# Eight more score halves fetched at the switch between two stages of a four-layer graph network, into tiles that the first stage has done with

## The chip, the core and the metric

The kernel runs on one core of a Trainium2 chip. The metric is the device time of one execution in microseconds (us), as the median of several runs. A profile is one execution with the hardware profiler on; its span goes from the first to the last instruction, and the execution's own time is a little longer.

The engines are PE (matmul), DVE (vector), ACT (activations), POOL (GpSimd) and SP, which here only issues DMAs. All large transfers of this kernel are issued by SP and share the core's 16 DMA engines.

## What is computed

The reference applies four graph layers with a residual each to `x` of 128 batches x 128 nodes x 128 features, with an integer adjacency `adj`. The change concerns the second layer, whose attention scores come from the absolute difference of every pair of nodes:

```python
D = jnp.abs(x[:, :, None, :] - x[:, None, :, :])
h = jnp.einsum('bijc,oc->bijo', D, W1) + b1          # 64 outputs for each pair
m = jnp.mean(h, axis=(0, 1, 2))
v = jnp.mean((h - m) ** 2, axis=(0, 1, 2))           # over ALL batches and pairs
h = (h - m) / jnp.sqrt(v + EPS) * g1 + be1
h = _leaky(h)
s = jnp.einsum('bijo,uo->biju', h, W2)[..., 0] + b2[0]
A = jax.nn.softmax(jnp.where(A_init > 0, s, NEG), axis=-1)
```

The mean and variance run over all batches, so no score can be finished before `h` of every pair is known. The kernel therefore computes `h` for all batches in a first stage and comes back to it in a second one.

## The kernel before, in words

**First stage.** The 128 batches stand in 32 groups of four (`G` = 4, `NG` = 32, `NB` = 128). For each group a "chain" (`chain(g)` in the first stage, lines 427 to 549) does layer one with tiles `x`, `adj`, `mask`, `hn`, `hT`, `maskT`, `hw`, `o` and `h1` of pool `p0`. For each batch, `pairs(i)` (lines 378 to 401) makes four steps `i`: a difference of 128x2048 in a tile `d` (two tiles for DVE, two for POOL: tags `d0` and `d1`, two buffers each, line 322), its absolute value on ACT, the product with `W1` on PE, a copy from PSUM on ACT into a half of a tile `z`, and statistics on DVE. Two steps fill one half of a batch: 128x2048 float32, 1 MB, 8 KB a partition. The half is written to DRAM (`HP`, line 359). The halves live in a ring of `FETCHED` = 10 tiles `z` (line 656).

**The order.** The steps of the first stage carry an engine, a cost, their predecessors and a rank. `_ranked` lays them out in one order, and each engine's instructions stand in it in that order. SP is one such queue: an instruction that waits on it holds back all that stand behind it.

**The switch.** The last four batches (n = 0 to 3 in the order of the second stage) are never written to DRAM: their eight halves stay in the ring. The step `fetch` (line 686) fetches the next batch (n = 4: two halves, `HP[0]`) into the two tiles left. In between stands a short block of small instructions (lines 727 to 762) that turns the statistics into `scale1` and `bias1`.

**Second stage.** It runs in slots, `slot(b)` (lines 843 to 877) with b from -1 on, in an order written out by hand. Slot b prepares batch b + 1 on ACT (`z0`, line 850, and `zr`, line 854) and DVE (`z0`, line 868), multiplies batch b on PE (line 825, 24 matmuls), copies the sums of batch b - 1 (`su`, line 846), brings them into order on PE (line 832) and adds them to `sk` (lines 839, 841). Then it fetches one batch, b + 5, into the two ring tiles that batch b has just left (lines 875 and 876, `fetch` at line 658, the DMA at line 662).

Every four slots one group's scores are complete, and a "turn" of the second stage's own `chain(turn)` (lines 879 to 977) does the rest of layer two for it, with its steps placed at fixed slots. For turn k: in slot 4k + 5 SP writes `sk` to DRAM (`rows<-sk`, line 902) and loads `x` (line 905); in slot 4k + 7 SP reads the scores back in another layout (`u<-rows`, line 909), which waits until `rows` has landed; in slot 4k + 9 DVE normalises `x` (line 244) and folds `u` (line 920); in slot 4k + 10 PE transposes `u` (line 894) and DVE makes the scores (lines 924, 925); in slots 4k + 11 to 4k + 16 softmax and products follow, with tiles `hT`, `aT` and `yT` (line 897). The result goes to DRAM (lines 957, 958), except for the groups of turns 27 to 31 (`KEPT` = 5), whose `Y` and `X1` stay on chip in a pool `keep` of ten small tiles.

From slot 12 to slot 38 some steps of `brief()` (preparations for the last stage) stand in the slots too; in slots 21 to 36 these are two maxima over a byte mask on DVE in each slot.

**Last stage.** Layers three and four, group by group, behind a condition computed on the way (`bounded`). The functions `last_stage` and `two_stages(True)` belong to branches of which the profile has no instruction.

Of the kernel before, what the change touches and what calls it, by code (L numbers as in the profile page):

```python
# [9 lines left out]
F32 = mybir.dt.float32  # L10
# [7 lines left out]
P = 128  # L18
G = 4
# [9 lines left out]
KC = 8  # L29
ROW = P + 2 * KH  # L30
# [3 lines left out]
NT = KH // KC  # L34
KEPT = 5
# [134 lines left out]
def tile_gnn_stack(ctx: ExitStack, tc: tile.TileContext, a: dict, out: bass.AP):  # L170
    nc = tc.nc
    NB = a["x"].shape[0]
    NG = NB // G
# [5 lines left out]
    psum, banks, Y, X1 = None, {}, {}, {}  # L179
# [44 lines left out]
    MV1 = res.tile([P, NG, G, 2], F32, name="MV1")  # L224
# [41 lines left out]

    def two_stages(general):
        nonlocal psum, banks
        early, middle, early_ring = (ExitStack() for _ in range(3))
        psum = early.enter_context(tc.tile_pool(name="psum", bufs=1, space=bass.MemoryType.PSUM))  # L270
        banks = {"sm": 2}
        ahead_by = FETCHED - 2 * general
# [1 line left out]
        with tc.tile_pool(name="c0", bufs=1) as c0, tc.tile_pool(name="p0", bufs=2) as p0:  # L274
# [42 lines left out]
            def difference(i):  # L317

                b, t = divmod(i, NT)
                xe, k = XE[b // 2], b % 2  # L320
                on_pool = t in ON_POOL
                d = p0.tile([P, 2, KC, P], F32, tag=f"d{int(on_pool)}", bufs=2 - general, name="d")
                x = xe[:, k, 0:P] if on_pool else XP[b // 2 % 2][:, k, :]
                ahead = xe[:, k, 1 + KC * t:]
                ahead = bass.AP(tensor=ahead.tensor, offset=ahead.offset,
                                ap=[list(ahead.ap[0]), [KH, 2], [1, KC], [1, P]])
                eng = nc.gpsimd if on_pool else nc.vector
                eng.tensor_tensor(d, ahead, x[:, None, None, :].to_broadcast([P, 2, KC, P]),  # L328
                                  OP.max if t == BY_MAX else OP.subtract)
                diffs[i] = d.rearrange("p h k i -> p h (k i)")  # L330
# [96 lines left out]
            def chain(g):  # L427
# [4 lines left out]
                own = lambda *names: [(name, g) for name in names]  # L432

                def tile0(name, dtype=F32, **kw):
                    t[name] = p0.tile([P, G, P], dtype, tag=name, name=name, **kw)
                    return t[name]

                def loaded():
# [70 lines left out]

                def h1(half):  # L510
                    if g not in H1:
                        H1[g] = p0.tile([P, G, P], F32, name="h1", bufs=3)
                    for k in (2 * half, 2 * half + 1):
                        nc.scalar.activation(H1[g][:, k, :], t["x"][:, k, :], AF.Relu, bias=t["nb"][:, k:k + 1],
                                             scale=t["rs"][:, k:k + 1])
# [129 lines left out]
            if general:  # L645
# [3 lines left out]
                steps.clear()  # L649
                relations()  # L650

            ring = early_ring.enter_context(tc.tile_pool(name="ring", bufs=1, side="right"))
            fetched = []

            def held_z():
                return ring.tile([P, NT // 2 * KC * P], F32, tag="z", bufs=ahead_by, name="z")

            def fetch(n):

                if n < 2 * NB:  # L660
                    b, half, z = n // 2 - G, n % 2, held_z()
                    nc.sync.dma_start(z, HP[b][:, half * NT // 2:(half + 1) * NT // 2, :].rearrange("p a b -> p (a b)"))
                    fetched.append(z)

            def first_fetches():
                fetched.extend(halves[b, half] for b in range(NB - G, NB) for half in range(2))
                for n in range(2 * G, ahead_by):
                    fetch(n)

            pick = fixed([P, 2, 8], F32, name="pick")  # L670
            nc.gpsimd.tensor_copy(pick.rearrange("p h (a c) -> p h a c", a=2),
# [11 lines left out]
                chain(g)  # L683
            for i in range(NT * NB):
                pairs(i)
            step("fetch", "SP", 0.8, [("hs", NT * NB - 2), ("st", NT * NB - 2 * NT), ("out", NB - G - 1)], NT * NB, first_fetches)
            later = []

            def in_const(name, *parts, n=P, shape=None):
# [73 lines left out]


        early.close()
        if not general:
            keep = ctx.enter_context(tc.tile_pool(name="keep", bufs=1))
            for g in range(NG - 1 - KEPT, NG - 1):
                Y[g], X1[g] = (keep.tile([P, G, P], F32, name=f"{n}{g}") for n in ("y", "x1"))
        psum = middle.enter_context(tc.tile_pool(name="psum2", bufs=1, space=bass.MemoryType.PSUM, reuse_waits="tile"))  # L770
        banks = {"ps": 3, "pk": 2, "sm": 3}
        with tc.tile_pool(name="c1", bufs=1, reuse_waits="tile") as c1, \
                tc.tile_pool(name="p1", bufs=2, reuse_waits="tile") as p1:
            prepared, scored = {}, {}

            z0 = c1.tile([P, 1], F32, name="z0")
            nc.vector.scalar_tensor_tensor(z0, bias1, 0.01, bias1, op0=OP.mult, op1=OP.max)
# [65 lines left out]
            def slot(b):  # L843
                if b - 1 in scored:
                    su = p1.tile([P, 4, P], F32, name="su")
                    nc.vector.tensor_copy(su.rearrange("p a b -> p (a b)"), scored[b - 1])  # L846
                    scored[b - 1] = su, sm("pk", "pk")
                if b + 1 < NB:
                    z0, z1 = fetched.pop(0), fetched.pop(0)
                    nc.scalar.activation(z0, z0, AF.Identity, bias=bias1, scale=scale1[:, 0:1])  # L850
                now(b, "am")
                if b + 1 < NB:
                    zr = p1.tile([P, NT // 2 * KC * P], F32, name="zr", bufs=3)
                    nc.scalar.activation(zr, z1, AF.Relu, bias=bias1, scale=scale1[:, 0:1])  # L854
                    prepared[b + 1] = z0, z1, zr
                now(b, "e")
                if b in prepared:
                    z0b, z1b, zrb = prepared.pop(b)
                    ps = psum.tile([P, 512], F32, tag="ps", bufs=banks["ps"], name="ps")
                    products(ps, [(w2z, z0b)], 0)  # L860
                    products(ps, [(w2l, z1b)], 4)
                if b - 1 in scored:
                    by_k(b - 1)
                if 0 <= b < NB:
                    products(ps, [(w2r, zrb)], 4)
                    scored[b] = ps
                if b + 1 < NB:
                    nc.vector.scalar_tensor_tensor(z0, z0, 0.01, z0, op0=OP.mult, op1=OP.max)  # L868
                now(b, "p")
                now(b, "a")  # L870
                if b - 1 in scored:
                    to_sk(b - 1)
                now(b, "l")
                if 0 <= b < NB:
                    fetch(2 * b + ahead_by)
                    fetch(2 * b + ahead_by + 1)
                now(b, "s")

            def chain(turn):
# [14 lines left out]
                        nc.tensor.transpose(t[name][:, k, :], src[:, k, 0:P], ident)  # L894

                def copied(name, src):
                    t[name] = p1.tile([P, G, P], F32, tag=name, name=name)
                    nc.scalar.copy(t[name], t[src])

                def to_rows():  # L900
                    to = rows[0, 0, 0:1]
                    nc.sync.dma_start(bass.AP(tensor=to.tensor, offset=to.offset,
                                              ap=[[ROW + 1, P], [P * ROW, G], [1, 1 + 2 * KH]]), own_sk)
                    t["x"] = p1.tile([P, G, P], F32, name="x", bufs=3)
                    nc.sync.dma_start(t["x"], X[g])

                def from_rows():
                    t["u"] = p1.tile([P, G, ROW], F32, name="u")
                    nc.sync.dma_start(t["u"], rows.rearrange("g i r -> i g r"))

                def normed():
                    t["h"] = pre_norm(p1, t["x"], MV1[:, g], RS1[:, g])
                    t["cap"] = p1.tile([P, G, P], F32, name="cap")
                    nc.gpsimd.tensor_scalar(t["cap"], M8[g], BIG, NEG12, op0=OP.mult, op1=OP.add)
                    t["x1"] = X1[g] if g in Y else p1.tile([P, G, P], F32, name="x1", bufs=3)
                    nc.gpsimd.tensor_tensor(t["x1"], t["x"], over_group(bt), OP.add)  # L916

                def folded():
# [1 line left out]
                    nc.vector.tensor_tensor(u[:, :, 0:2 * KH], u[:, :, 0:2 * KH], u[:, :, P:], OP.add)  # L920

                def scores():
                    t["e"] = p1.tile([P, G, P], F32, name="e1")
                    nc.vector.tensor_tensor(t["e"], t["u"][:, :, 0:P], t["put"], OP.add)
                    nc.vector.tensor_tensor(t["e"], t["e"], t["cap"], OP.min)

# [21 lines left out]
                    nc.tensor.matmul(t["pz"], wgT, t["yT"], start=True, stop=True)  # L948

                def biased():  # L950
                    t["y"] = Y[g] if g in Y else p1.tile([P, G, P], F32, name="y")
                    nc.scalar.activation(t["y"], t["pz"], AF.Identity, bias=bg)

                def stored():
# [168 lines left out]


        middle.close()
        early_ring.close()

    two_stages(False)
# [4 lines left out]
    def last_stage():  # L1133
        nonlocal psum, banks
        with tc.tile_pool(name="c2", bufs=1) as c2, tc.tile_pool(name="p2", bufs=5) as p2, \
# [84 lines left out]
            def group(g):  # L1220
# [27 lines left out]
                for k0 in range(0, G, 2):  # L1248
# [13 lines left out]
                    yield from last_of(softmax(pes), got)  # L1262
                    eTs = []
                    for e in got[0]:
                        eT = p2.tile([P, 4, P], F32, name="eT", bufs=12)
                        transpose(eT, e)
                        eTs.append(eT)
                        yield
# [26 lines left out]
                sums = small.tile([P, 1, G], F32, name="sums3")  # L1295
                got = []
                yield from last_of(softmax([pe], sums), got)
                eT = p2.tile([P, 4, P], F32, name="eT", bufs=12)
                transpose(eT, got[0][0])
                nc.vector.reciprocal(sums, sums)  # L1300
                yield
# [332 lines left out]
```

## Time and profile before

| | |
|---|---|
| median of 3 runs | 2674.77 us (2673.55 to 2675.49) |
| the profiled execution: its own time | 2676.09 us |
| its span | 2674.2 us, mean granted PE clock 0.98 |
| busy share: PE, DVE, ACT, POOL | 91%, 92%, 89%, 64% |
| moved by DMA | 611.43 MB; read 312.58 MB, written 296.03 MB |
| fetches `z<-hp` / writes `hp<-z` | 248 each, 1024 KB each, median 13.7 / 4.0 us from issue to landing |
| `u<-rows`, `rows<-sk` | 32 each, 384 KB and 130 KB, median 11.4 and 13.0 us |
| last result copy of the first stage on ACT (line 352) | starts at 1450.6 us |
| first preparation on ACT (line 850) | starts at 1459.3 us |
| first and last batch's first matmul (line 825) | 1463.8 and 2211.2 us |
| first instruction of the last stage on ACT (line 1373) | 2247.03 us |

In a row of the profile, `L825 PE MATMUL ps<-z,w2z` is line 825, its engine, operation, and the tile written and those read; `SPq` is SP issuing a DMA. "Idle <-X" is the time that the engine stood idle just before, and what ended it. A row such as `DVE u L920 <- DMA u<-rows: 30.0, 17, 5.7` of the view of waits reads: who waited for whom, us in all, times, the longest. The view of windows gives for each stretch of time the busy us of each engine (and instructions), the granted PE clock, the mean busy share of the DMA engines and GB/s.

### The profile page before, as it was taken

Reading aid. Unit: us, or ns where it says so; the run is one execution under the profiler, and the core shown is the slowest. Engines: PE = TensorE matmul, PEld = TensorE weight load, DVE = VectorE, ACT = ScalarE, POOL = GpSimd, SP = SyncE. Lnnn points to the kernel's source line nnn. Section 1 sums busy time; section 2 is a strip of 40 time slices with the busy share of each in tenths; the row PEclk is TensorE's granted clock in tenths of the full one; section 3 lists DMA queues with packets and bytes.
Section 4 is the critical chain, followed back from the end, with each engine's and each line's share of the span. In section 5 each row is a group of like instructions: output and inputs, shape, how many; then the busy total and the mean of one; then the engine's idle time right before and its main releaser. Section 6 shows DMA issues by size and latency. Waiting matters only on the chain.

```text
span 2674.2 us, 41925 instructions
## 1 busy us (share of the span) xinstructions
PE 2437.0 (91%) x14521; PEld 1162.1 (43%) x14521; DVE 2469.6 (92%) x4738; ACT 2380.3 (89%) x2821; POOL 1706.1 (64%) x1628
## 2 busy tenths in 40 slices
PE   6999999999999999999997988888888886999997
PEld 3333333333333333333332443444444445777776
DVE  5999999999999999999998789988888886899997
ACT  5999999999999999999998877788778874999997
POOL 6999999999999999999985000010101123666663
PEclk8999999999999999999998999999999998999999
DMA  3555555555555555555542999999999992021211
GB/s 101 201 206 209 212 212 211 212 213 205 209 205 209 205 210 204 217 204 216 205 197 93 409 409 384 392 409 410 411 410 411 410 373 81 21 68 56 64 37 34
DMA packets 185426, 611.43 MB, mean 229 GB/s; under 512 B 31987, under 2 KB 99702, under 8 KB 121718
## 3 DMA queue, kind: packets, MB, share of 16 engines
q1 hardware_dynamic: 184768, 608.50, 59.1%
q8 instruction: 118, 1.93, 0.3%
q14 instruction: 102, 0.84, 0.1%
q10 hardware_dynamic: 438, 0.17, 0.0%
HBM read 312.58 MB, written 296.03 MB: 228 GB/s over the span
## 4 chain that ended last, share of the span: by engine, by line
PE 37%; ACT 24%; DVE 15%; DMA 12%; POOL 7%; issue 4%; SPq 0%; POOLq 0%; DVEq 0%; ACTq 0%
PE hp L338 16%; ACT d L376 9%; ACT z L352 7%; DMA z<-hp 4%; PE hp L341 4%; DMA rows<-sk 4%; PE ps L825 4%; POOL d L328 4%; DMA u<-rows 3%; DVE z L868 3%; ACT o L473 2%; PE pk L832 2%; ACT hn L473 2%; PE xp L414 1%; DVE e L1502 1%
## 5 line engine op out<-in xcount | busy, mean ns | idle before, releaser
L328 POOL TENSOR_TENSOR d<-xe 128x2048 f32<-128x2048 f32 x256 | 1073.8, 4205 | 36.4 <-PE hp L338 34.5
L338 PE MATMUL hp<-d,w1T 128*64 128x512 f32 x4096 | 994.1, 601 | 57.6 <-ACT z L352 54.5
L376 ACT ACTIVATE d<-d 128x2048 f32<-128x2048 f32 x384 | 733.8, 1924 | 19.8 <-POOL d L328 19.5
L328 DVE TENSOR_TENSOR d<-xe,xp 128x2048 f32<-128x2048 f32 x256 | 583.6, 2280 | 7.0 <-POOL xe L423 4.0
L352 ACT COPY z<-hp 128x1024 f32<-128x1024 f32 x512 | 519.1, 1015 | 9.7 <-PE hp L338 4.5
L338 PEld LDWEIGHTS hp<-d,w1T 128*64 128x64 f32 x4096 | 276.9, 136 | 559.5 <-issue 455.3
L916 POOL TENSOR_TENSOR x<-x,bt 128x512 f32<-128x512 f32 x32 | 48.8, 1525 | 665.7 <-DMA x<-x 494.1
L366 DVE BATCH_NORM_STATS2 st<-z 128x6 f32<-128x512 f32 x512 | 354.7, 693 | 6.2 <-ACT z L352 6.1
L367 DVE BATCH_NORM_STATS2 st<-z 128x6 f32<-128x512 f32 (+1 forms) x512 | 336.4, 657 | 0.0
L868 DVE SCALAR_TENSOR_TENSOR z<-z 128x2048 f32<-128x2048 f32 x128 | 299.5, 2340 | 5.5 <-ACT z L850 5.3
L850 ACT ACTIVATE z<-z,bias,scale 128x2048 f32<-128x2048 f32 x128 | 267.5, 2090 | 8.9 <-DVE bias L762 7.7
L854 ACT ACTIVATE zr<-z,bias,scale 128x2048 f32<-128x2048 f32 x128 | 267.7, 2092 | 0.5 <-DMA z<-hp 0.5
L341 PE MATMUL hp<-both_t,xw 128*64 128x512 f32 x1024 | 265.2, 592 | 0.0
L825 PE MATMUL ps<-z,w2z 128*32 128x512 f32 x1024 | 140.9, 622 | 61.2 <-DVE z L868 60.5
L832 PEld LDWEIGHTS pk<-pick,su 128*128 128x128 f32 x1024 | 126.8, 195 | 147.8 <-DVE su L846 112.9
L832 PE MATMUL pk<-pick,su 128*128 128x16 f32 x1024 | 139.4, 268 | 34.6 <-DVE su L846 33.8
L825 PE MATMUL ps<-zr,w2r 128*32 128x512 f32 x1024 | 142.5, 629 | 0.0
L341 PEld LDWEIGHTS hp<-both_t,xw 128*64 128x64 f32 x1024 | 77.6, 137 | 142.2 <-issue 142.2
L825 PE MATMUL ps<-z,w2l 128*32 128x512 f32 x1024 | 138.4, 610 | 0.0
L1525 PE MATMUL pv<-wr,e 128*128 128x128 f32 x1024 | 134.0, 278 | 2.1 <-ACT wr L1450 1.1
L1525 PEld LDWEIGHTS pv<-wr,e 128*128 128x128 f32 x1024 | 124.1, 192 | 8.4 <-ACT wr L1450 1.8
L1409 ACT ACTIVATE h<-x,nb,rs 128x128 f32<-128x128 f32 x256 | 106.0, 491 | 20.1 <-POOL nb L1404 18.4
(241 smaller groups left out, 3808.3 us busy)
## 6 DMA issues: line engine op xcount, KB each, us to landing
hp<-z SPq DMA_DIRECT2D x248, 1024.0 KB, 4.0
z<-hp SPq DMA_DIRECT2D x248, 1024.0 KB, 13.7
x<-x SPq DMA_DIRECT2D x118, 256.0 KB, 4.8
u<-rows SPq DMA_DIRECT2D x32, 384.0 KB, 11.4
x<-in_x_dram SPq DMA_DIRECT2D x32, 256.0 KB, 5.6
adj<-in_adj_dram SPq DMA_DIRECT2D x32, 256.0 KB, 5.9
out_dram<-x SPq DMA_DIRECT2D x32, 256.0 KB, 2.4
z<-y SPq DMA_DIRECT2D x27, 256.0 KB, 11.8
```

What stands on the lines that cost most here:

```text
L328: eng.tensor_tensor(d, ahead, x[:, None, None, :].to_broadcast([P, 2, KC, P]), OP.max if t == BY_MAX else OP.subtract)
L338: nc.tensor.matmul(hp[64 * hh:64 * hh + 64, c:c + 512], w1T2 if by_max else w1T, d[:, hh, c:c + 512], start=True, stop=not by_max, skip_gr ...
L341: nc.tensor.matmul(hp[64 * hh:64 * hh + 64, c:c + 512], XW[i // NT // 2][:, i // NT % 2, :], both_t.rearrange("p h k i -> p h (k i)")[:, h ...
L352: nc.scalar.copy(half_of(b, t), linear.pop(i))
L366: nc.vector.bn_stats(st[:, 2 * t, :], hs[:, 0:512])
L367: nc.vector.bn_stats(st[:, 2 * t + 1, :], hs[:, 512:1024 - P * last])
L376: nc.scalar.activation(diffs[i], diffs[i], AF.Abs)
L825: nc.tensor.matmul(ps[32 * c:32 * c + 32, :], w[:, w0:w0 + 32], v[:, 512 * c:512 * c + 512], start=j0 == 0, stop=w is w2r, skip_group_chec ...
L832: nc.tensor.matmul(pk[:, kk, 0:16], su[:, kk, :], pick.rearrange("p h j -> p (h j)"), start=True, stop=True)
L850: nc.scalar.activation(z0, z0, AF.Identity, bias=bias1, scale=scale1[:, 0:1])
L854: nc.scalar.activation(zr, z1, AF.Relu, bias=bias1, scale=scale1[:, 0:1])
L868: nc.vector.scalar_tensor_tensor(z0, z0, 0.01, z0, op0=OP.mult, op1=OP.max)
```

## The change

It lets eight more halves be fetched at the switch. The first stage's chain tiles move into a pool of their own, `upper`, and the difference tiles into another, `spare`. Once the last group's chain is done, four halves (n = 4 and 5) are fetched over the chain tiles; the ring's two free tiles take n = 6; and as the last four differences are used up, four halves (n = 7 and 8) go into the tiles `d`. So five batches are asked for ahead of slot 0 instead of one.

In the slots the fetches are rearranged (`refill`): slots 0 to 3 fetch n = 9 to 12, slots 4 and 5 nothing, slot 6 n = 13, slot 7 n = 14 (into two of the tiles `d`, from here on called the pair), slot 8 nothing, slot 9 n = 15, and so on with n = b + 6; every sixth slot from 14 to 104 uses the pair. Slot 110 fetches nothing, and from slot 111 on n = b + 5. After slot 5 the space of the chain tiles goes to the turns (`x`, `u`, `hn`, `cap`, `x1`, `e1`, `y`); after slot 8 two of the tiles `d` serve as `hT`, `aT`, `yT` (two of each) and as two of the ten kept tiles; after slot 110 the pair holds the other eight.

The number of instructions of SP, PE and ACT's and DVE's large ones is the same. In the built order, SP's four fetches over the chain tiles stand ahead of the two last writes of the first stage (`hp123`); POOL's first `cap` stands behind `scale1` instead of ahead of it; and DVE's `w2r` and `add_k` stand after line 754 of before instead of among lines 736 to 739.

```diff
-                d = p0.tile([P, 2, KC, P], F32, tag=f"d{int(on_pool)}", bufs=2 - general, name="d")
+                d = room["d"].tile([P, 2, KC, P], F32, tag=f"d{int(on_pool)}", bufs=2 - general, name="d")
...
-                    t[name] = p0.tile([P, G, P], dtype, tag=name, name=name, **kw)
+                    t[name] = room["chain"].tile([P, G, P], dtype, tag=name, name=name, **{"bufs": 2} | kw)
...
+            room = {"d": p0, "chain": p0}
+            if not general:
+                room["d"] = ctx.enter_context(tc.tile_pool(name="spare", bufs=1, side="right"))
             ring = early_ring.enter_context(tc.tile_pool(name="ring", bufs=1, side="right"))
-            fetched = []
+            if not general:
+                room["chain"] = upper.enter_context(tc.tile_pool(name="upper", bufs=1, side="right"))
+            fetched, asked = {}, itertools.count(G)
...
-            def fetch(n):
-                if n < 2 * NB:
-                    b, half, z = n // 2 - G, n % 2, held_z()
-                    nc.sync.dma_start(z, HP[b][:, half * NT // 2:(half + 1) * NT // 2, :].rearrange("p a b -> p (a b)"))
-                    fetched.append(z)
+            def fetch(pair):
+                n = next(asked)
+                if n < NB:
+                    fetched[n] = pair = [next(pair), next(pair)]
+                    for half, z in enumerate(pair):
+                        nc.sync.dma_start(z, HP[n - G][:, half * NT // 2:(half + 1) * NT // 2, :].rearrange("p a b -> p (a b)"))
+            in_ring = (held_z() for _ in itertools.count())
+            def spares():
+                for _ in range(2):
+                    for tag in ("d0", "d1"):
+                        yield room["d"].tile([P, 2, KC, P], F32, tag=tag, bufs=2, name="z").rearrange("p h k i -> p (h k i)")
+            in_spares = (z for _ in itertools.count() for z in spares())
+            def upper_pool(name):
+                upper.close()
+                return upper.enter_context(tc.tile_pool(name=name, bufs=1, side="right", reuse_waits="tile"))
+            def upper_fetches():
+                room["chain"] = None
+                pool = upper_pool("upper_z")
+                pairs = (pool.tile([P, NT // 2 * KC * P], F32, name=f"z{n}") for n in range(4))
+                fetch(pairs)
+                fetch(pairs)
             def first_fetches():
-                fetched.extend(halves[b, half] for b in range(NB - G, NB) for half in range(2))
-                for n in range(2 * G, ahead_by):
-                    fetch(n)
+                fetched.update({b - NB + G: [halves[b, 0], halves[b, 1]] for b in range(NB - G, NB)})
+                for n in range(2 * G, ahead_by, 2):
+                    fetch(in_ring)
+            def spare_fetches():
+                fetch(in_spares)
+                fetch(in_spares)
...
+                step("upper", "SP", 0.8, [("xp", 2 * g), ("xp", 2 * g + 1), ("h1", g, 0), ("h1", g, 1), ("x", g)], NT * NB, upper_fetches)
+                step("spare", "SP", 0.8, ["fetch", ("hp", NT * NB - 1)], NT * NB, spare_fetches)
+            step("fetch", "SP", 0.8, [("hs", NT * NB - 2), ("st", NT * NB - 2 * NT), ("out", NB - G - 1)] + in_upper, NT * NB, first_fetches)
...
-            keep = ctx.enter_context(tc.tile_pool(name="keep", bufs=1))
-            for g in range(NG - 1 - KEPT, NG - 1):
-                Y[g], X1[g] = (keep.tile([P, G, P], F32, name=f"{n}{g}") for n in ("y", "x1"))
...
+            def lent(turn, name, n):
+                if general:
+                    return p1.tile([P, G, P], F32, tag=name, name=name)
+                return small_ones[2 * n + turn % 2]
...
+            def refill(b):
+                if general:
+                    fetch(in_ring)
+                elif b == G + 4:
+                    small_ones.extend(in_four(next(in_spares)) + in_four(next(in_spares)))
+                    kept_ones = iter(small_ones[6:] + in_four(pair[0]) + in_four(pair[1]))
+                    for g in range(NG - 1 - KEPT, NG - 1):
+                        Y[g], X1[g] = next(kept_ones), next(kept_ones)
+                elif b == G + 3:
+                    pair.extend((next(in_spares), next(in_spares)))
+                    fetch(iter(pair))
+                elif b in range(G + 10, NB - 4 * G, 6):
+                    if b + 6 < NB - 3 * G:
+                        fetch(iter(pair))
+                elif b not in (G, G + 1):
+                    fetch(in_ring)
...
                 if 0 <= b < NB:
-                    fetch(2 * b + ahead_by)
-                    fetch(2 * b + ahead_by + 1)
+                    refill(b)
+                if b == G + 1 and not general:
+                    room["turns"] = upper_pool("turns")
...
-                    t[name] = p1.tile([P, G, P], F32, tag=name, name=name)
+                    t[name] = lent(turn, name, ("hT", "aT", "yT").index(name))
...
-                    t["u"] = p1.tile([P, G, ROW], F32, name="u")
+                    t["u"] = room["turns"].tile([P, G, ROW], F32, name="u", bufs=2)
...
-                        eT = p2.tile([P, 4, P], F32, name="eT", bufs=12)
+                        eT = p2.tile([P, 4, P], F32, name="eT", bufs=11)
```

The other tiles of a turn are moved from `p1` to `room["turns"]` in the way of `u`; `eT` is a tile of `last_stage`.

## Prediction

> **What bounds the kernel now.** I read the page's slices first, then the view of windows around the switch, then the waits of DVE and ACT in the second stage, and last the chain and the timelines of SP and DVE at the places that those named. In the slices, second-stage DMA (from the 23rd slice) stands at 9 and at some 410 GB/s, and the two slices ahead of it fall away:
>
> ```profile
> DVE  5999999999999999999998789988888886899997
> DMA  3555555555555555555542999999999992021211
> GB/s 101 201 206 209 212 212 211 212 213 205 209 205 209 205 210 204 217 204 216 205 197 93 409 409 384 392 409 410 411 410 411 410 373 81 21 68 56 64 37 34
> ```
>
> Windows show the hole and the rates after it (last two figures of a row: DMA share, GB/s):
>
> ```profile
> 1420.00:1430.00 10.00, 8.95 (x42) 3.13 (x40) 9.31 (x12) 9.15 (x7) 8.62 (x3) 1.00 0.03 11
> ...
> 1450.00:1460.00 10.00, 1.96 (x10) 1.20 (x7) 6.54 (x28) 1.67 (x2) 0.81 (x2) 0.76 0.00 0
> ...
> 1620.00:1690.00 70.00, 57.75 (x428) 28.22 (x432) 66.95 (x109) 50.03 (x37) 4.76 (x5) 0.95 1.00 374
> 1690.00:1850.00 160.00, 141.60 (x1107) 68.35 (x1099) 141.70 (x224) 130.85 (x91) 21.12 (x14) 1.00 1.02 407
> 1850.00:2190.00 340.00, 298.22 (x2267) 142.84 (x2266) 287.33 (x442) 270.73 (x188) 44.63 (x28) 0.98 1.03 410
> ```
>
> DMA moves next to nothing from 1420 to 1465, then all it can. But who waits for it? DVE's waits from 1455 to 2212, then ACT's from 1500 to 2200:
>
> ```profile
> DVE e L924 <- PE pt L894: 45.9, 30, 2.3
> DVE u L920 <- DMA u<-rows: 30.0, 17, 5.7
> ```
> ```profile
> ACT z L850 <- DMA z<-hp: 1.2, 2, 0.8
> ACT zr L854 <- DMA z<-hp: 0.5, 1, 0.5
> ```
>
> The fetched halves are hardly ever late (1.7 us in all). What is late is `u`, which stands behind them in the same DMA queue. The chain of the longest such wait:
>
> ```profile
> 1486.24 14.93 DMA rows<-sk
> ...
> 1501.24 11.35 DMA u<-rows
> ...
> 1512.61 0.43 DVE u L920
> ```
>
> The 30.0 us lie in three stretches: 5.7 at 1512; 0.9 in two waits up to 1558; none from there to 1850; then 23.5 in 14 turns. The gap from 1558 to 1850 has a cause: the slots with the byte maxima keep DVE busy 66.95 of 70 us, DMA falls to 374 GB/s, and halves land some 7 us after issue near 1653 (13 to 14.5 near 1550 or 2000): the queue has run empty. It then fills slowly. A turn's DMA is 8 x 1.05 MB + 0.13 + 0.39 + 3 x 0.26 = 9.7 MB, 23.7 us at 410 GB/s; unhindered engines take 22.3 (first matmuls of batches 52 and 64: 1771.6, 1838.6). So the queue grows by 1.4 us a turn until `u` is late.
>
> **The change part by part.**
>
> *Earlier fetches.* Eight halves at 1.05 MB / 410 GB/s = 2.56 us are 20.5 us of DMA. Four may start once the last transposes to `xp` are done (1405.4), two after the last write (now at 1412.1; the four ahead of it in the queue cost it 10 us, to about 1421), and four as the last products free `d` (1444 to 1451). All land by about 1457, before ACT's 1459.3. The hole hides them; differences on DVE took 2.25 to 2.29 us at 1414 (358 GB/s) as at 1428 (11 GB/s), so I charge stage one nothing. No later step of stage one waits for the delayed `hp123`.
>
> *Slots 0 to 8.* In before they run at 3.95 us each without a wait for data (first matmuls: 1463.8 for batch 0, 1495.7 for batch 8). More data in hand makes them no faster. What changes is the queue: slots 0 to 3 issue the same eight halves as before (1465.8 to 1478.4, landed by 1490.2), then slots 4, 5 and 8 issue nothing. In before:
>
> ```profile
> 1478.35 7.77 SPq L662 DMA_DIRECT2D z<-hp  x5
> 1486.24 0.37 SPq L902 DMA_DIRECT2D rows<-sk  x1
> ...
> 1501.24 0.37 SPq L909 DMA_DIRECT2D u<-rows  x1
> ```
>
> Behind it `rows` took 14.9 us to land, with SP held at `u` until then, and `u` 11.35. Now at 1486 only 4 us are queued; `rows` lands near 1491, `x` (0.6 us) by 1492, and SP isn't held. Two batches (slots 6, 7; first issue 1488.9) take 4 x 2.56, to 1502; `u`, issued near 1496, lands at about 1503 to 1504. DVE can fold from about 1505 (it did its work ahead of line 920 by 1507, with 0.9 us lost to `x`). The wait goes. What is late next is the engines' own pace: batches 8 to 12 took 28.5 us; the turn after it (12 to 16) took 22.6 with 0.3 of wait. That is 5.9; slots 9 to 12 alone took 24.5 against 17.6 for the same phase later (45 to 48): 6.9. I take 6.5. Here a rule bears: the Trainium skill (TensorE: Matmul & The Clock Gate, What's actually happening) says that PE drops to half clock after an idle window of about 3.4 us. The record agrees (half clock for 3.4 + 6.8 us between 1506 and 1520). By the rule alone I would add 10.2 x 0.5 = 5.1 us to the 6.6 of waits: 11.7; the turn's measured excess already holds both, so the row decides.
>
> *After slot 9.* The order on SP is still two halves in each slot, freed by that slot's products, only one batch further on. So rows and `u` meet the same queue, and the maxima empty it in both kernels. Of the 20.5 us of lead, 5.1 are thus kept as a sixth batch in hand, and what goes beyond that and the 6.5 is given back as DMA idle time in slots 4 to 9 and 21 to 37. The rule that speaks for more is the Trainium skill's Perfetto Trace Analysis (Optimization Strategy): a gap that repeats can mean too few buffers for the next tile. By it the sixth batch would take the 23.5 us after 1850 too. But that gap waits for `u`, not for a tile `z`: by the row, zero. I take zero between slots 9 and 109.
>
> *Slot 110.* It fetches nothing: 5.1 us leave the queue, which regrows by 1.4 a turn, so the next three waits should vanish:
>
> ```profile
> 2135.79 0.43 DVE L920 TENSOR_TENSOR u<-u 128x256 f32<-128x256 f32 x1 [1.39 <-DMA u<-rows]
> 2160.09 0.43 DVE L920 TENSOR_TENSOR u<-u 128x256 f32<-128x256 f32 x1 [2.55 <-DMA u<-rows]
> 2183.79 0.43 DVE L920 TENSOR_TENSOR u<-u 128x256 f32<-128x256 f32 x1 [2.12 <-DMA u<-rows]
> ```
>
> 6.1 us of waits; by turns (batches 112 to 124: 23.5, 24.3, 23.7 against 22.4 each) 4.3. I take 4.5; bounds 2 and 6.
>
> *Small moves.* DVE's `w2r` and `add_k` (0.19 + 0.16 us) now stand between lines 754 and 758, where DVE idles 1.0 us for POOL's `scale`: nothing, 0.4 if the cover fails. POOL's `cap` (0.62) moves behind `scale`, waits for slot 5's products, and only `x1` is queued behind it, needed ten slots later: nothing. The load of `x` in slot 5 waits on SP for products of that slot; behind it stands slot 6's fetch, which waits for later products anyhow. Shared tiles could add waits where dependencies are kept per tile: `hT`, `aT`, `yT` are rewritten after products that PE's order already puts first: nothing, at most 1 us at the last stage's start, or as much less with the tiles elsewhere. `eT` and the general path are in branches without an instruction in the profile.
>
> **The sum.** 6.5 + 4.5 = 11.0 us. The profiled execution would take 2676.09 - 11.0 = 2665.1; the median of before is 1.3 under its profile, so 2663.8. With the bounds (5.9 to 6.9, 2 to 6, small moves up to 1.4 lost): 7 to 13 us, 2662 to 2668.
>
> **The rivals.**
> 1. *DMA is the bound, and all 20.5 us count.* For it: 410 GB/s flat, and a turn's DMA (23.7) longer than its engines' pace (22.3). Against: no wait for `z`, and 70 us at 374 GB/s, where a lead cannot be kept. 2674.8 - 20.5 = 2654.3. Chance 0.15.
> 2. *Only one end works.* If the relief of slot 110 is eaten by rows already queued: 2668.3 (0.09). If turn 0's `u` is still late, because SP meets it behind two fetched batches: 2670.3 (0.08), no change that can be told.
> 3. *Slower: the sixth batch lengthens the queue that `u` stands in.* If more than two halves could be issued in a slot, `rows` and `u` would each be 5.1 us later from turn 1 on: 10.2 at slot 13, whose wait now is 0.3, and the waits after 1850 begin four turns sooner, 4 x 1.3 = 5.2; less 6.5: +8.9, 2683.7. It decides once a slot's issue runs ahead of its products. For it: z takes 13.7 us to land already. Against: SP's order. Chance 0.06.
>
> The forecast itself has 0.62. A measurement here can tell about 0.2% (5.3 us) from no change. Faster by more: 0.62 + 0.15 + 0.09, less 0.02 for the low end; within: 0.10; slower: 0.06. The range 2654 to 2670.5 takes in rivals 1 and 2.
>
> **What would show it.** Right: GB/s near 400 in 1406 to 1425 and again at 1445 to 1457; the wait of line 920 near 1505 gone, with batch 12's first matmul near 1517.5; DMA well under 400 GB/s in part of 1486 to 1510 and still low in the maxima's stretch; waits for `u` from about 1845 to slot 109 as large as now; none after. Wrong: waits after 1850 vanished (rival 1), or a wait of line 920 at slots 9 or 13 (rivals 2, 3); or a later start than 1459.3 of the second stage.

## The result and the profile after

The kernel after takes 2660.58 us (median of 6, 2658.9 to 2664.41), before took 2674.95 on the same chip: a ratio of 0.9947, with a 95% interval of 0.9934 to 0.996. That is 14.4 us less, against 11.0 forecast. The profiled execution of after took 2658.9 us, its span is 2657.1, 17.1 less than before's. It is the fastest of after's six, so its distances are 2 to 3 us larger than those of the medians.

The slices of the page of after, for DVE, DMA and GB/s:

```profile
DVE  5999999999999999999998899988888886899997
DMA  3555555555555555555545999999999992022211
GB/s 104 200 206 210 209 210 210 212 211 209 210 210 210 209 211 209 210 207 212 207 195 222 365 408 374 395 409 408 411 409 410 404 359 80 21 69 57 65 37 34
```

The hole in the 22nd slice is filled (93 to 222 GB/s). From the 24th slice on the rates are nearly those of before. The windows (last figures: PE clock, DMA share, GB/s):

```profile
1410.00:1420.00 10.00, 9.13 (x44) 3.03 (x42) 10.00 (x14) 9.08 (x8) 7.89 (x3) 1.00 1.01 419
1420.00:1430.00 10.00, 8.95 (x42) 3.13 (x40) 9.32 (x12) 8.79 (x8) 8.32 (x3) 1.00 0.69 243
1440.00:1450.00 10.00, 8.31 (x38) 2.78 (x34) 6.59 (x14) 8.79 (x8) 3.86 (x1) 1.00 0.70 231
1450.00:1460.00 10.00, 1.98 (x8) 1.72 (x8) 6.31 (x31) 2.21 (x3) 0.81 (x2) 0.68 0.49 190
1620.00:1690.00 70.00, 60.91 (x439) 29.38 (x435) 65.22 (x109) 51.98 (x37) 5.70 (x6) 0.93 1.00 375
1690.00:1850.00 160.00, 141.92 (x1110) 68.47 (x1106) 141.46 (x218) 131.19 (x92) 17.83 (x13) 1.00 1.03 408
```

The DMA now moves the eight halves in this stretch. The first of these windows in before:

```profile
1410.00:1420.00 10.00, 9.13 (x44) 3.21 (x44) 10.00 (x13) 9.32 (x8) 8.03 (x2) 1.00 0.94 358
```

From 1410 to 1430 PE and DVE do as much as before (PE 9.13 and 8.95 us in the two windows of either kernel, DVE 10.00 and 9.3), and batch 0 starts at 1462.3 us (1463.8 before): the fetches cost stage one nothing that can be seen.

SP's timeline where turn 0's scores go out and come back:

```profile
1482.52 0.37 SPq L966 DMA_DIRECT2D rows<-sk  x1
1482.94 0.50 SPq L969 DMA_DIRECT2D x<-x  x1
1487.35 5.19 SPq L669 DMA_DIRECT2D z<-hp  x4
1492.63 0.39 SPq L973 DMA_DIRECT2D u<-rows  x1
```

`u` is asked for at 1492.6 instead of 1501.2, and DVE folds it as soon as it gets there (no wait in brackets), as announced. That is the first of the next three rows. The others are the last wait for `u` in after, in slot 109, and a fold two turns later, again without a wait:

```profile
1503.35 0.42 DVE L984 TENSOR_TENSOR u<-u 128x256 f32<-128x256 f32 x1
...
2099.59 0.43 DVE L984 TENSOR_TENSOR u<-u 128x256 f32<-128x256 f32 x1 [0.79 <-DMA u<-rows]
...
2145.00 0.42 DVE L984 TENSOR_TENSOR u<-u 128x256 f32<-128x256 f32 x1
```

Over the whole stage DVE waits 20.3 us for `u` where it waited 30.0. All of it lies from 1860 to 2100. In before there are eleven such waits from 1850 to slot 109, and eleven in after (17.4 and 20.3 us). What has gone are the three waits up to 1558 (6.6 us) and the three behind slot 110 (6.1):

```profile
DVE e L988 <- PE pt L958: 49.8, 31, 3.4
DVE u L984 <- DMA u<-rows: 20.3, 11, 2.7
```

By first matmuls, after is ahead by 1.0 us at batch 8, 10.3 at batch 12 (slots 8 to 11 take 19.2 us where they took 28.5), 12.0 at 24, 11.4 at 36, 11.7 at 68, 10.9 at 108 and 15.6 at 127. So the gain comes at the two ends and little is added between, as the forecast had it. The question is why it is these two amounts.

### The profile page after: what moved, and what is told of

Read it like the earlier page. It is cut to its first block, busy times and chain, and to the rows that moved or that the text cites. A ratio compares the mean times of both kernels' runs of the same rounds, so it can differ in the third digit from the quotient of the medians.

```text
span 2657.1 us, 41953 instructions
## 1 busy us (share of the span) xinstructions
PE 2429.4 (91%) x14521; PEld 1160.3 (44%) x14521; DVE 2467.9 (93%) x4738; ACT 2376.7 (89%) x2821; POOL 1704.3 (64%) x1628
## 2 busy tenths in 40 slices
DMA packets 185427, 611.43 MB, mean 230 GB/s; under 512 B 31988, under 2 KB 99703, under 8 KB 121719
## 5 line engine op out<-in xcount | busy, mean ns | idle before, releaser
L980 POOL TENSOR_TENSOR x<-x,bt 128x512 f32<-128x512 f32 x27 | 39.8, 1473 | 551.7 <-DMA x<-x 482.2
L366 DVE BATCH_NORM_STATS2 st<-z 128x6 f32<-128x512 f32 x512 | 348.2, 680 | 4.4 <-ACT z L352 4.3
L367 DVE BATCH_NORM_STATS2 st<-z 128x6 f32<-128x512 f32 (+1 forms) x512 | 329.7, 644 | 0.0
L1567 DVE SCALAR_TENSOR_TENSOR e<-e,ps 128x512 f32<-128x512 f32 x160 | 106.8, 675 | 10.7 <-ACT ps L1564 10.3
## 6 DMA issues: line engine op xcount, KB each, us to landing
z<-hp SPq DMA_DIRECT2D x248, 1024.0 KB, 11.1
u<-rows SPq DMA_DIRECT2D x32, 384.0 KB, 11.5
```

Source lines behind the costliest of these rows:

```text
L366: nc.vector.bn_stats(st[:, 2 * t, :], hs[:, 0:512])
L367: nc.vector.bn_stats(st[:, 2 * t + 1, :], hs[:, 512:1024 - P * last])
```

## The experiments

Two theories. **The queue theory** is the forecast's: `u` stands in SP's queue behind the halves, its lateness is what costs, and the lead beyond two repaired waits runs into DMA idle time. **The volume theory** is its first rival: the second stage is paced by all the bytes that it has to move, and whoever waits for a DMA only shows that pace. To keep apart what it says, I split each profile's time of batch 127's first matmul into four terms: 1465 us, the bytes moved from there to the end of the full flow at 410.5 GB/s, the idle time of the DMA in between, and the tail from the flow's end to that matmul. The flow's end is found in steps of 2 us, so terms are good to about 2 us at best. The split is arithmetic and proves nothing alone; it says which term an edit moved. In before the DMA is idle for 12.2 of the 733 us up to the flow's end, so little can be gained there without moving bytes out or shortening the tail.

| kernel | bytes | DMA idle | tail | batch 127 | median, us | ratio to before (95%) |
|---|---|---|---|---|---|---|
| before | 720.8 | 12.2 | 13.2 | 2211.2 | 2674.95 | 1 |
| after | 701.4 | 15.6 | 13.6 | 2195.6 | 2660.58 | 0.9947 (0.9934 to 0.996) |
| 1 chain tiles only | 710.9 | 12.1 | 13.8 | 2201.8 | 2665.43 | 0.9971 (0.9961 to 0.9981) |
| 2 difference tiles only | 711.4 | 13.6 | 15.7 | 2205.7 | 2668.69 | 0.9986 (0.9978 to 0.9994) |
| 3 relief at 86 | 699.3 | 15.7 | 17.2 | 2197.2 | 2660.13 | 0.9949 (0.9935 to 0.9963) |
| 4 before, rows sooner | 721.9 | 7.1 | 7.5 | 2201.5 | 2664.59 | 0.997 (0.9959 to 0.9981) |
| 5 after, rows sooner | 701.4 | 17.6 | 7.8 | 2191.8 | 2655.69 | 0.9931 (0.9918 to 0.9943) |
| 6 after, rows on POOL | 699.6 | 17.4 | 15.7 | 2197.7 | 2660.9 | 0.9947 (0.9932 to 0.9963) |
| 7 before, rows on POOL | 721.8 | 7.2 | 8.8 | 2202.8 | 2665.5 | 0.9965 (0.9952 to 0.9978) |
| 8 after, maxima spread | 701.1 | 7.9 | 16.0 | 2190.0 | 2653.83 | 0.9931 (0.9917 to 0.9945) |
| 9 sooner and spread | 700.9 | 10.1 | 13.2 | 2189.2 | 2648.53 | 0.9904 (0.9891 to 0.9917) |
| 10 after, few maxima | 700.3 | 10.7 | 18.4 | 2194.4 | 2654.87 | 0.9926 (0.9913 to 0.994) |

The medians of before beside 1 to 4, 5 to 7 and 8 to 10 were 2672.59, 2673.54 and 2672.78 us, so ratios compare better than medians.

Number 3 shows what a single profile is worth. Up to slot 86 it has the same instructions in the same order as after, and yet its batch 68 came at 1855.3 us where after's came at 1849.4, and its first wait for `u` at 1934 where after's came at 1861. Its terms differ from after's by up to 3.6 us. Smaller differences between two rows of the split say nothing.

**1. Chain tiles only.** Only the four halves over the chain tiles are fetched early; there is no sixth batch.

```diff
             def spare_fetches():
-                fetch(in_spares)
-                fetch(in_spares)
+                pass
...
-                elif b == G + 3:
-                    pair.extend((next(in_spares), next(in_spares)))
-                    fetch(iter(pair))
-                elif b in range(G + 10, NB - 4 * G, 6):
-                    if b + 6 < NB - 3 * G:
-                        fetch(iter(pair))
                 elif b not in (G, G + 1):
                     fetch(in_ring)
```

> Only the four halves over the dead chain tiles are fetched early (n = 4, 5); the tiles d take no fetch, slot 8 fetches again, and from slot 6 on each slot fetches b + 5, slot 110 too. Queue theory (u of a turn is late because of the halves ahead of it in the DMA queue; what pays is the gap of slots 4 and 5 at the start and of slot 110 at the end): the gain of the start is whole (9 us between batches 8 and 12, no wait for u there), that of the end is gone: waits for u of about 2 us a turn come back in slots 113 to 121. 2665.5 us. Volume theory (each half moved out of the stage in which DMA is busy all the time is worth the same, 14.4 us for eight): half the halves, half the gain, 2667.7 us.

**2. Difference tiles only.** Only the four halves in the tiles `d`; the sixth batch stays until slot 108.

```diff
             def upper_fetches():
...
-                pool = upper_pool("upper_z")
-                pairs = (pool.tile([P, NT // 2 * KC * P], F32, name=f"z{n}") for n in range(4))
-                fetch(pairs)
-                fetch(pairs)
+                upper_pool("upper_z")
...
-                elif b == G + 4:
+                elif b == G + 2:
...
-                elif b == G + 3:
+                elif b == G + 1:
...
-                elif b in range(G + 10, NB - 4 * G, 6):
-                    if b + 6 < NB - 3 * G:
+                elif b in range(G + 8, 109, 6):
+                    if b < 108:
                         fetch(iter(pair))
-                elif b not in (G, G + 1):
+                else:
```

> Only the four halves into the tiles d are fetched early (n = 5, 6), the chain tiles take none; slots 0 to 5 and 7 fetch, slot 6 does not, the sixth batch of lead is kept to slot 108. Queue theory: rows of turn 0 stand behind twelve halves as in the kernel before and land near 1501, but only slot 7's two halves stand between them and u instead of four, so the wait of 5.7 us shrinks to about 1; the end keeps its gain: 2662.5 us. Volume theory: half of 14.4, 2667.7 us.

Measured: 7.2 and 3.9 us less than before by the medians (7.8 and 3.7 by the ratios). Number 1 lies too near both expectations to tell them apart; batch 12 came at 1513.9 us as in after, and there are waits for `u` down to the end. Number 2 falls short of both: batch 12 came at 1517.9, 6.3 us earlier than in before, but at slot 108 only 0.8 were left; then the relief brought it to 5.5. The two together give 11.1 of the 14.4 us, a difference that the intervals (2.7 and 2.1 us each way, 3.5 for after) don't rule out as chance. In the split both moved 9 to 10 us of bytes out of the stage, and number 2 lost 4 of them to idle time and tail, about as much as two profiles can differ by chance. The waits for `u` don't rank the kernels. Numbers 1 and 2, from the views of DVE's waits:

```profile
DVE u L978 <- DMA u<-rows: 17.5, 16, 1.6
```
```profile
DVE u L981 <- DMA u<-rows: 14.1, 13, 3.0
```

Number 2 waits less for `u` than after (20.3) and than number 1, and takes longer than either.

**3. Relief at 86.** The kernel after, with the slot that fetches nothing at 86 instead of 110.

```diff
-                elif b in range(G + 10, NB - 4 * G, 6):
-                    if b + 6 < NB - 3 * G:
+                elif b in range(G + 10, 87, 6):
+                    if b < 86:
```

> The changed kernel, but the sixth batch is given up in slot 86 instead of 110 (slot 86 fetches nothing, from 87 on b + 5). Queue theory: the same time within 1.5 us, 2660.6: the waits for u of the turns after slot 86 (slots 89, 93, 97) vanish and those of slots 113 to 121 are back at 1.4 to 2.6 us each. Rival (the gain of the end comes from the stage's last transfers being over sooner): 2664.5 to 2665.

It takes what after takes. The waits for `u` are gone from 1958 to 2072 and come back from 2073 to 2168 (five, up to 3.5 us). The queue theory's picture of a relief that lasts a few turns holds, and the end doesn't care where it is placed.

**4. Before, with the rows one slot sooner,** and with them `x` and `u`. No byte is moved out of the stage.

```diff
-                at(G * turn + G + 1 - final, "s", to_rows)
-                at(G * turn + G + 3 - 2 * final, "s", from_rows)
+                at(G * turn + G, "s", to_rows)
+                at(G * turn + G + 2 - final, "s", from_rows)
```

> The kernel BEFORE, no fetch moved, but rows, x and u of every turn are issued one slot sooner (slots 4k + 4 and 4k + 6). Queue theory: u of turn 0 lands about when it is needed (wait 0 to 1.5 instead of 5.7), worth about 8; the waits from slot 68 on begin four turns later (5.6 us of slack against 1.4 us a turn), worth about 4.5: 2662.5 us, nearly the whole gain of the change with not one byte moved. Volume theory: the same bytes in the same stage, 2675 us.

8.0 us less, so the volume theory in its bare form (bytes alone) is wrong: order in the queue counts. It is two thirds of what the queue theory asked for, and the split shows in which terms it lies: 5.1 us less DMA idle time, and a tail that is 5.7 shorter. And there is a new wait. From the views of DVE's and ACT's waits:

```profile
DVE u L920 <- DMA u<-rows: 18.9, 11, 3.8
```
```profile
ACT z L850 <- DMA z<-hp: 10.6, 15, 1.5
ACT zr L854 <- DMA z<-hp: 4.6, 9, 0.8
```

ACT now waits 15.2 us for halves, where it waited 1.7 in before. I therefore restated the volume theory: batch 127 comes at the stage's bytes, plus DMA idle time, plus tail; an edit counts by the term that it moves. Numbers 5 to 10 were expected from that.

**5. After, with rows, `x` and `u` one slot sooner** (from turn 1 on).

```diff
-                at(G * turn + G + 1 - final, "s", to_rows)
-                at(G * turn + G + 3 - 2 * final, "s", from_rows)
+                sooner = turn > 0
+                at(G * turn + G + 1 - sooner, "s", to_rows)
+                at(G * turn + G + 3 - sooner - final, "s", from_rows)
```

> The kernel after, with rows, x and u of the turns from 1 on issued one slot sooner; no byte is moved. Pacing by u alone (the queue regrows by 1.35 us a turn, a slot sooner is 3.95 us of slack, so the waits of DVE for u begin some three turns later): 3 x 1.35 = 4 us, 2656.5. Pacing by the stage's DMA (the gain is DMA idle time saved between 1465 and 1700 plus a last batch closer to the last transfer): the same edit made before's idle time there shrink from 10.0 to 4.7 us and its tail shorter by about 5, and after has 12.5 us of such idle time, so about 5 to 8 and up to 3: 2650 to 2655.5.

2655.69 lies between the two expectations; by the ratio it is 2656.5, the queue theory's number. With 3.2 us each way it doesn't tell them apart. The idle time did not shrink as I expected from number 4 (17.6); the tail did (7.8), as there.

**6 and 7. Rows and `u` in a queue of their own**, issued by GpSimd, in after and in before. This takes `u` out from behind the halves altogether.

```diff
-                    nc.sync.dma_start(bass.AP(tensor=to.tensor, offset=to.offset,
+                    nc.gpsimd.dma_start(bass.AP(tensor=to.tensor, offset=to.offset,
...
-                    nc.sync.dma_start(t["u"], rows.rearrange("g i r -> i g r"))
+                    nc.gpsimd.dma_start(t["u"], rows.rearrange("g i r -> i g r"))
```

> The kernel after, with rows and u issued by GpSimd in a queue of its own, so that u no longer stands behind the fetched halves; the same bytes. Pacing by u alone: all waits for u go, 11 turns x 1.35 us = 14 to 15, 2646 (ACT does not wait for z, or hardly). Pacing by the stage's DMA: the DMA has no idle time between 1700 and 2180 to give, so ACT's waits for z take the place of DVE's waits for u (10 us or more in all), and only idle time saved before 1700 and a shorter tail count, 3 to 8 us: 2653 to 2657.5.

> The kernel before with rows and u in GpSimd's queue; no byte is moved out of the stage. Pacing by u alone: turn 0's 6 to 9 us and the 14 waits after 1850 at 1.35 each, 19, so 25 to 28 us: 2647 to 2650. Pacing by the stage's DMA: no hole is filled, so turn 0's gain is lost again later and only idle time (10.0 us between 1465 and 1700, and the tail of 14) can be saved: 8 to 12 us, 2663 to 2667, with ACT waiting for z from about 1950 on.

This decides against the queue theory. In both kernels DVE no longer waits for `u` at all, and neither time came near the queue theory's: 2660.9 against 2646, and 2665.5 against 2647 to 2650. Nor is a gain merely lost again at the start: from batch 68 to batch 127, where the waits for `u` stood, number 7 took 346.3 us and before 350.1, number 6 343.9 and after 346.1. That is 3.8 and 2.2 us less, where the queue theory asked for 19 and for 14 to 15; the 6 us by which two profiles can differ don't bridge that. What waits instead, in number 7 on ACT and DVE, and in number 6 on DVE:

```profile
ACT z L850 <- DMA z<-hp: 30.8, 35, 2.5
ACT zr L854 <- DMA z<-hp: 11.0, 16, 1.4
DVE hn L244 <- DMA x<-x: 15.3, 12, 2.9
```
```profile
DVE hn L244 <- DMA x<-x: 5.6, 6, 2.4
```

With `u` out of the way, what shares SP's queue is late: in number 7 the halves and `x`, in number 6 `x` alone. In number 7 `x` is already 2.9 us late for turn 0, and slots 8 to 11 took 26.9 us, against 28.5 in before. The same window in before, after, number 7 and number 6, in this order:

```profile
1968.00:2158.00 190.00, 166.41 (x1284) 80.23 (x1276) 161.49 (x250) 151.16 (x105) 27.49 (x16) 0.99 1.03 410
```
```profile
1968.00:2158.00 190.00, 164.59 (x1270) 78.66 (x1264) 162.53 (x250) 150.97 (x105) 30.27 (x18) 0.99 1.02 408
```
```profile
1968.00:2158.00 190.00, 162.68 (x1262) 77.32 (x1261) 165.24 (x248) 152.87 (x105) 27.30 (x32) 1.00 1.02 409
```
```profile
1968.00:2158.00 190.00, 165.91 (x1264) 78.96 (x1264) 165.08 (x249) 150.20 (x105) 27.36 (x32) 0.98 1.02 410
```

Last column 408 to 410 and engines busy alike, whoever waits. Number 7 gains by the same terms as number 4 (idle 7.2, tail 8.8). Number 6 missed my own range by 3 us: it gained no idle time, and ACT, which I expected to wait 10 us or more for halves, waited for none. So where number 6 loses what DVE no longer waits is not shown. Its `rows` and `u` stand in POOL's order now, with POOL's `cap` and `x1` behind them, and its batch 12 came 2.1 us later than after's; whether that is the reason was not tried. The edit has one more effect: in both kernels the profile has 156755 DMA packets where before has 185426 and after 185427, for the same 611.4 MB, so not only the place in the queue has changed.

**8 to 10. The DMA's idle time itself.** In after 7.4 of the 15.6 us lie between 1600 and 1680, under the byte maxima (0.676 us each, two a slot, 21.6 us in all). Number 8 puts them at one a slot; 9 has the edit of 5 as well; 10 leaves 30 of the 32 out (the maximum over the adjacency is then that of two groups only).

```diff
-                searched = end + 9 + NG // 2
+                searched = end + 9 + NG
...
-                    at(end + 9 + g // 2, "l", lambda g=g: highest(g))
+                    at(end + 9 + g, "l", lambda g=g: highest(g))
```

Number 10, against after:

```diff
-                    nc.vector.tensor_reduce(t["tops"][:, NG:NG + 1], t["tops"][:, 0:NG], AX.X, OP.max)
+                    nc.vector.tensor_reduce(t["tops"][:, NG:NG + 1], t["tops"][:, 0:2], AX.X, OP.max)
...
-                for g in range(NG):
+                for g in range(2):
                     at(end + 9 + g // 2, "l", lambda g=g: highest(g))
```

> The kernel after with the 32 byte maxima at one a slot (slots 21 to 52) in place of two a slot (21 to 36); the same instructions and bytes. If the DMA of the stage paces it, the idle time of the DMA counts: of the 15.6 us between 1465 and the end of its flow some 8 lie between 1600 and 1680, under the maxima at two a slot. At one a slot a turn costs DVE 2.7 us less there, so engines and DMA go at nearly one pace and 5 to 8 us of the idle time go: 2653 to 2656. If the waits for u pace it, the engines' work up to 1850 is the same, only later, and the queue empties as much: 2659 to 2662.

> Both edits: rows, x and u one slot sooner from turn 1 on, and the maxima at one a slot. If the DMA paces the stage they save different terms (the way from the last byte to the last batch, and DMA idle time), so they add up: 2655.7 less 5 to 8, 2648 to 2651. If u paces it: 2655 to 2657, as with rows sooner alone.

> The kernel after without 30 of the 32 byte maxima (the maximum over the adjacency is left out for the groups from 2 on), so 30 x 0.676 = 20.3 us of DVE work are gone. It gives the most that the maxima can cost. If the DMA paces the stage, only its idle time counts, 6 to 9 us: 2652 to 2655. If the engines' pace before 1700 counts whole (the four turns from batch 24 to 40 took 24.7, 27.4, 26.2 and 24.1 us against 22.3, an excess of 13.2): 2647 to 2649.

By the medians all three fell into the ranges of the volume theory and outside those of its rival. Before was some 2 us faster beside them than beside after, so the ratios are the stricter measure: by these, numbers 8 and 10 gained 4.3 and 5.6 us on after, a little less than the 5 to 8 and 6 to 9 that I expected, and still far from the rival's 0 and 12. The window of the maxima in number 8, and in number 10:

```profile
1620.00:1690.00 70.00, 62.62 (x465) 29.49 (x463) 65.25 (x105) 54.68 (x39) 5.97 (x6) 0.95 1.03 410
```
```profile
1620.00:1690.00 70.00, 61.84 (x462) 29.21 (x461) 61.30 (x99) 52.83 (x39) 8.49 (x6) 0.95 1.02 409
```

375 GB/s have become 410 and 409: the idle time in this window is gone. The intervals of numbers 8 and 10 overlap after's a little. Number 8's profile has 7.7 us less idle time and 2.4 more tail. Number 10's profile, its slowest execution, has 4.9 less and 4.8 more, so it doesn't show the gain of the medians. Leaving 20.3 us of DVE work out (number 10) gained no more than moving it, within the noise: the amount of DVE's work was not what counted, and the DMA's idle time is what both edits removed.

Number 9 is the fastest, 0.9904: 24.3 us below before and, by the ratios, some 11.5 below after. Its interval lies apart from those of before, after and number 5. Against number 5, which lacks only the spread maxima, it gained 7.2 us by the ratios, the clearest sign that spreading them pays. But its terms are not those that I expected to add up: against after it has 5.5 us less idle time and hardly less tail (0.4), so the shorter tail of number 5 is not seen in it.

## Why the forecast came out as it did

The time fell within the forecast's range, which takes in two of the rivals, and on its side, 3.2 us under its number. The 14.4 us lie beyond the bounds that the forecast gave its own sum (7 to 13). Most steps held; one reason and two sizes did not. Of the signs, the filled stretches came at 386 and 309 GB/s (1406 to 1425 and 1445 to 1457), the second below the announced 400; 1486 to 1510 fell to 368 as announced.

*Earlier fetches free for stage one:* right (batch 0 at 1462.3, 419 GB/s from 1410 to 1420 with DVE busy throughout).

*Turn 0's wait, 6.5 us:* right in mechanism, too small. The turn from batch 8 to 12 gained 9.3. I measured its excess against the next turn and against slots 45 to 48. Unhindered, slots 8 to 11 took 19.2 us and not 22. By the program's order they hold the engines' steps of the first turn only, where later slots hold those of two; that this is the reason was argued and not tried. The sum by the clock rule of the Trainium skill (TensorE: Matmul & The Clock Gate, What's actually happening), 11.7, which I put aside, was off by about as much the other way. (The 3.95 us a slot that I read up to slot 8 are 3.99 on average, which changes nothing here.) The half clock of 1506 to 1520 did vanish: behind the start of the stage (half clock to 1467.2) after's first such stretch starts at 1559.4.

*Zero between slots 9 and 109:* right as a number (10.3 us ahead at batch 12, 10.9 at 108), wrong as a reason. I argued that the late transfer is `u` and not a `z`, so that more halves in hand can't help. In number 7 the wait for `u` is only where the DMA's pace comes to light; remove it and `z` and `x` are late at the same 408 to 410 GB/s, and number 6 gains as little. The gain doesn't grow in this stretch because the DMA runs at its rate in both kernels. That it also stays so level from batch to batch is in part chance: by number 3's batch 68 the lead there would be 5.8 us. The rule that I set aside there, the Trainium skill's Perfetto Trace Analysis (Optimization Strategy), says that a repeated gap can mean too few buffers; by it the 23.5 us of waits after 1850 would have gone, but with the sixth batch in hand, up to slot 109, all eleven are left (17.4 us in before, 20.3 in after). Neither its reading nor mine named the byte rate.

*Slot 110, 4.5 us:* right. From batch 108 to 127 after gained 4.7, with no wait for `u` behind slot 109; number 3 moved the relief and its pause without changing the total.

*The rest "given back as DMA idle time in slots 4 to 9 and 21 to 37":* this is the term that was mis-sized. With 20.5 us moved, of which 5.1 stay in hand up to slot 110 and 6.5 are kept, it had to be 8.9; the split shows 3.4 us more idle time than before (12.2 to 15.6): 0.9 from 1490 to 1520, 1.2 from 1600 to 1620, 1.1 at the relief from 2100 to 2150, and none from 1620 to 1690 (374 and 375 GB/s). So 19.4 less 3.4 and 0.4 of tail, 15.6 us, arrive at batch 127. I had charged the lead with idle time that before had too (374 GB/s in the maxima's stretch).

*Rival 1* (all 20.5 us, 2654.3) had the right bound and went too far by 6.3 us; idle time accounts for 3.4 of them. I argued against it with the missing waits for `z`. *Rival 2:* in after itself turn 0 gained 9.3 and the end 4.7, so neither end failed. *Rival 3:* no wait in slots 9 or 13, and no more waits after 1850 than before.

Still open: why number 2 kept only 3.9 us; why the tail is 7.5 to 8.8 us in numbers 4, 5 and 7 and 13 to 18 in the rest, number 9 with its sooner rows among them; and why number 5 gained no idle time where 4 did.

## What to carry to other kernels

When a stage moves bytes at one flat rate almost without a break, take that rate as its pace, even if hardly anybody waits for the large transfers: here, in a shared queue, the transfer with the least slack was the one that showed up late, and when it was moved away the next one did. Cost an edit there by bytes moved out of the stage, less the idle time that the lead adds, plus what it does to the way from the last byte to the end. Then look for stretches inside the stage where the rate dips; here engine work taken out of such a stretch paid although it was put back elsewhere. And before reading small differences, compare two profiles of the same instructions.

## What was unexpected of the hardware

A queue of its own did not bring `u` in quickly: its median from issue to landing fell only from 11.5 us behind the halves (after) to 7.9 on GpSimd's queue (number 6), and the halves' rose from 11.1 to 14.7, at the same total rate.

The granted clock did not rank these kernels. Between 1465 and 2212 us PE ran at half clock for 29.5 us in after, 40.4 in number 8 and 47.3 in number 10. By span number 8 is 5.1 us shorter than after (2652.0 against 2657.1) and number 10 the same (2656.8). I had expected dips of the clock to show in the times; in the sum over this stage they don't, as far as one profile of each can tell.
